# A decoder layer on one core: the first keys fetched by halves, and the FFN turned so that its inner features lie on partitions

## The chip, the cores and the metric

The kernel runs on one core of one Trainium2 chip. The metric is the device time of one execution in microseconds (us). TensorE (PE) multiplies, VectorE (DVE), ScalarE (ACT) and GpSimd (POOL) work elementwise, and SyncE (SP) issues most of the DMAs. Each engine runs its own instructions in order. SBUF is the on-chip memory of 128 partitions, PSUM the eight banks into which PE writes.

## The reference

Input x is 4 batches of 1024 tokens of 256 features; the context is 4 batches of 64 tokens. Everything is float32.

```
x = x + attn(LN(x))            # 16 heads of 16; softmax over 1024 keys, then / sqrt(256); biases
x = x + xattn(LN(x), ctx)      # 16 heads, 64 keys, scores / sqrt(16); biases
h = gelu(LN(x) @ T(W_fc).T)    # 1024 inner features
h = (h - mean(h)) * rsqrt(var(h) + 1e-5) * ln_w + ln_b     # over the 1024
x = x + h @ T(W_proj).T
LN(v) = (v - mean) / sqrt(var + 1e-5)
T(W)  = sign(W) * min(round(|W| / (mean|W| + 1e-6)), 1)    # entries -1, 0, 1
```

## The kernel before, in words

**Numbers in two parts.** Where a fast float32 product is wanted, a number is written as a rounded part and a rest (`hT` and `hl`, `xh` and `xl`), and both parts are multiplied.

**Start.** `load_x(0, 4)` (line 100) fetches batch 0 in four parts on SP's queue, then the query and key weights. `ln1(0)` normalises eight blocks of 128 tokens (lines 324 to 339), transposes them on PE into `xnT`, and `project(0, 0)` (line 341) makes queries and keys of the first eight heads. Their two parts are written to DRAM (`kept_q`, `kept_k`), and `fetch(u)` (line 368) reads them back in the layout that one unit needs: four heads, as two pairs, each of 64+64 rows. For each pair and side it issues four DMAs of 16 rows. On SP's queue a DMA also waits until an earlier one that holds the same semaphore has landed; for unit 0 half of the key DMAs are issued by ACT.

**Units.** There are 16 units (a batch and four heads). `maxima(u)` (line 412) multiplies queries by keys for 128 queries and 512 keys at a time, and DVE reduces each PSUM bank to a maximum (line 433). `turn_maxima` transposes these. In the main loop a step handles 128 keys and 512 queries: `scores` (line 872) multiplies the other way round, subtracts the maxima by a second product, and ACT takes the exponential (line 888); `weigh` (line 796) multiplies with the values. The maxima of the next unit run in the same steps. Sixteen maxima pieces of unit 0 come ahead of the loop (lines 861 to 864), with pieces of `values(0)` and `project(0, 1)` between them.

**Order.** PE and SP keep the order of the program (`ordered`). On the other engines a planner in the framework sets the order, so that an instruction may stand far ahead of its place in the program. Side work (`ln1`, `project`, `values` of the next batches; `post(b)`: output projection, cross attention and its norms; the weights' `ternary`) is written as generators, in three lines `due`, `later` and `aside`, that the steps advance by credits. `post(3)` is left over for the end.

**FFN** (lines 962 to 1106). The tokens are taken in eight halves of 512. `widen(i)` normalises four blocks, transposes them into `xh`, `xl`, and multiplies with the ternary `wfc`: per block of 128 tokens eight products of 512 inner features, so that tokens lie on partitions. ACT takes Gelu (line 1001), DVE the statistics (line 1004), ACT a square root; DVE and ACT then normalise two blocks each (lines 1012 and 1015). `narrow(i)` transposes h back (line 1031), ACT and DVE split it into `hT` and `hl` with the factor `lnw` (lines 1035, 1036), and PE multiplies with `wproj` into `py`. DVE adds `py` to x (line 1052), and SP writes it out. POOL adds `yrow`, the row that the layernorm's bias makes through `wproj` (line 280); `bias_row` (line 760) computes it in the main loop. The loop at line 1083 takes a piece of `post(3)` in two of five turns, and else a piece of `widen` or `narrow` by the places in `WIDE` and `NARROW` (line 1077); from the seventh half on, `widen` waits until `post(3)` is done.

Of the kernel before, what the change touches and what calls it, by code (L numbers as in the profile page):

```python
# [10 lines left out]
F32R = mybir.dt.float32r  # L11
DRAM = bass.MemoryType.DRAM
# [9 lines left out]
P = 128  # L22
# [8 lines left out]
def decoder_layer(ctx, tc, a, out):  # L31
# [39 lines left out]
    def load_x(b, n=1, view=x_view, slot=None):  # L71
        step = NT // n
        x_of[b] = x_slots[b % 3 if slot is None else slot]
        for i in range(n):
            sl = slice(i * step, (i + 1) * step)
            dma(
                out=x_of[b][:, sl, :], in_=view[:, b * NT + i * step : b * NT + (i + 1) * step, :]
            )
# [21 lines left out]
    load_x(0, 4)  # L100
    wqk = []
    for name in ("wq", "wk"):

        wide = main.tile([P, E // P, H, 32], F32, tag="q", name=f"{name}_in", bufs=4)
        dma(out=wide, in_=a[name].rearrange("(c p) (h e) -> p c h e", p=P, e=32))
        t = const.tile([P, E // P, H, D], F32, name=name)
        nc.gpsimd.tensor_copy(t, wide[:, :, :, 1 : 1 + D])
        wqk.append(t.rearrange("p c h e -> p c (h e)"))
# [13 lines left out]
    bo = load_row("bo")  # L122
    xbv = load_row("xbv")
    xbo = load_row("xbo")
# [37 lines left out]
    for i in range(3):  # L162
        t = (const if i else main).tile([P, NT, VW], F32, tag=f"v_sb{i}", name=f"v_sb{i}")
        nc.gpsimd.memset(t, 16.0)
        v_sb.append(t)

# [14 lines left out]
    state = {"split": False, "banks": "ring"}  # L181
# [47 lines left out]
    def ln_stats(pool, mv, blocks):  # L229

        for i, t in blocks:
            st = pool.tile([P, 6], F32, tag="bn", name="bn", bufs=3)
            nc.vector.bn_stats(out=st, in_=xs(t)[:, 0, :])  # L233
            nc.vector.bn_aggr(out=mv[:, i, :], in_=st)

    def ln_rstd(pool, rs, mv):
# [3 lines left out]
        nc.vector.reciprocal(out=rs, in_=sd)  # L240

    def ln_normalised(pool, mv, rs, i, t, n):
# [12 lines left out]
        for k in range(n):  # L255
            nc.vector.tensor_scalar(  # L256
                xn[:, k, :], xs(t + k)[:, 0, :], mv[:, i + k, 0:1], rs[:, i + k : i + k + 1],
                ALU.subtract, ALU.mult,
            )
# [108 lines left out]
    def fetch(u):  # L368
# [4 lines left out]
        for pair in range(2):  # L373
# [17 lines left out]
            for n in range(2):  # L391
                parts(k, kept_k, (0, 1, 0, 1), n, slice(0, S), dma if u or n else nc.scalar.dma_start)
# [19 lines left out]
    def maxima(u):  # L412
# [4 lines left out]
        for half in range(2):  # L417
            order = [(t, pair) for t in range(half * 4, half * 4 + 4) for pair in range(2)]
            if u == 0 and half == 0:

                order.sort(key=lambda at: at[1])
            for t, pair in order:
                q, k = qk_of[u][pair]
                for kh in range(2):
                    sides = two_banks()
                    for n, pm in enumerate(sides):
                        r = slice(64 * n, 64 * n + 64)
                        matmul(
                            pm, lhsT=q[r, t * P : (t + 1) * P],
                            rhs=k[r, kh * 512 : (kh + 1) * 512], start=True, stop=True,  # L430
                        )
                    for n, pm in enumerate(sides):
                        nc.vector.tensor_reduce(  # L433
                            mx[:, t, 2 * pair + n : 2 * pair + n + 1, kh], pm, AX.X, ALU.max
                        )
                    if kh == 1 and (t, pair) == order[-1]:
                        turning.append(turn_maxima(u, mx[:, half * 4 : half * 4 + 4, :, :]))
                    yield
# [281 lines left out]
    yrow = const.tile([P, E], F32, name="yrow")  # L720

# [37 lines left out]

    def bias_row():  # L760

        yield "free"
        wide = main.tile([P, HID // P, P], F32, tag="hl", name="lnb_wide", bufs=2)
        nc.gpsimd.tensor_copy(
            wide, late["lnb"].rearrange("p (c o) -> p c o", o=1).to_broadcast([P, HID // P, P])
        )
        yield "cols"
        pt = bank()
        w = ternaries[1].bitcast(F32)
        product(pt[:, 0:E], [(wide[:, c, :], w[:, c, :]) for c in range(HID // P)])  # L770
        nc.vector.tensor_copy(yrow, pt[:, 0:E])
# [50 lines left out]

    first, parts = ln1(0), project(0, 0)
    for _ in range(6):
        next(first)
# [4 lines left out]
    state["split"] = True  # L830
# [27 lines left out]

    due.add(values(0), 8)
    due.add(project(0, 1), 8)  # L860
    for i in range(16):
        top()
        if i % 3 != 0 and i < 15:
            due.step()
    run(turning.popleft())
    due.credit = 0.0
    load_x(1)
# [23 lines left out]
    for u in range(NU):  # L891
# [5 lines left out]
        if g == 0:  # L897
# [4 lines left out]
            for n in ((1, 2), (), (3,), ())[b]:  # L902
                if n > 1:
# [11 lines left out]
        if g == 1 and b == B - 1:  # L915
            aside.add(ternary("wfc", 2, HID), 10)
            aside.add(ternary("wproj", HID // P, E), 10)
            aside.add(bias_row(), 2)
        for step in range(2 * NT):
            half, kb = divmod(step, NT)  # L920
            if step < 2 and u + 1 < NU:
# [51 lines left out]
    h_of = {}  # L973
    NH = NT // 2

    def widen(i):
# [10 lines left out]
        h = ffn.tile([P, NH, HID], F32, tag="h", name="h", bufs=2)  # L987
        mv = ffn.tile([P, NH, 2], F32, tag="mvh", name="mvh", bufs=2)
        rs = ffn.tile([P, NH], F32, tag="rsh", name="rsh", bufs=2)
        h_of[i] = h  # L990
        for t in range(NH):
            yield "Gelu"
            ph = ps["wide"]()
            for half in range(2):
                for k in range(4):
                    c, part = divmod(k, 2)
                    matmul(
                        ph[:, half, :], lhsT=(xl, xh)[part][:, c, t * P : (t + 1) * P],
                        rhs=wfc[:, c, half * 512 : (half + 1) * 512], start=k == 0, stop=k == 3,
                    )  # L1000
            nc.scalar.activation(h[:, t, :], ph.rearrange("p a f -> p (a f)"), AF.Gelu)  # L1001
            st = ffn.tile([P, 2, 6], F32, tag="bnh", name="bnh", bufs=3)
            for half in range(2):
                nc.vector.bn_stats(out=st[:, half, :], in_=h[:, t, half * 512 : (half + 1) * 512])  # L1004
            nc.vector.bn_aggr(out=mv[:, t, :], in_=st)
        yield "Sqrt"
        ln_rstd(ffn, rs, mv)
        nmr = ffn.tile([P, NH], F32, tag="nmr", name="nmr", bufs=2)
        nc.vector.scalar_tensor_tensor(nmr, mv[:, :, 0], -1.0, rs, ALU.mult, ALU.mult)
        for t in range(0, NH, 2):  # L1010
            yield ""
            nc.vector.tensor_scalar(
                h[:, t, :], h[:, t, :], mv[:, t, 0:1], rs[:, t : t + 1], ALU.subtract, ALU.mult
            )
            nc.scalar.activation(
                h[:, t + 1, :], h[:, t + 1, :], AF.Identity, bias=nmr[:, t + 1 : t + 2],
                scale=rs[:, t + 1 : t + 2],
            )

    def narrow(i):  # L1020


        h = h_of.pop(i)
        t0 = i * NH
        py = ps["wide"]()
        parts = []
        for c in range(HID // P + 2):
            if c < HID // P:
                pt = bank()
                for n in range(NH):  # L1030
                    transpose(pt[:, n * P : (n + 1) * P], h[:, n, c * P : (c + 1) * P], ident)
                hT = ffn.tile([P, 512], F32R, tag="hT", name="hT", bufs=4)
                hl = ffn.tile([P, 512], F32R, tag="hl", name="hl", bufs=4)
                w = late["lnw"][:, c : c + 1]
                nc.scalar.activation(hT, pt, AF.Copy, scale=w)  # L1035
                nc.vector.scalar_tensor_tensor(hl, pt, w, hT.bitcast(F32), ALU.mult, ALU.subtract)  # L1036
                parts.append((hl, hT))
            if c >= 2:
                for k, part in enumerate(parts[c - 2]):
                    for n in range(NH):  # L1040


                        matmul(
# [120 lines left out]
```

## Time and profile before

| | us |
|---|---|
| three runs, median (lowest, highest) | 1367.08 (1364.13, 1367.55) |
| the profiled execution | 1365.17 |
| its span | 1363.4 |
| PE busy | 1282.1 (94%) |
| DVE busy | 1004.7 (74%) |
| ACT busy | 898.5 (66%) |
| POOL busy | 80.0 (6%) |

Busy shares are averages over stages with different limits, so they say little by themselves; a stage is read from the table of busy times by stretches and from what its engines wait for. A line of the timeline gives the start, the length, the engine, the line of the kernel, the operation with what it writes and reads, the count, and in brackets the idle time before it with what ended it. "issue" there means that no releaser is seen in the profile. Matmul ends are modelled and overlap, so the pitch from start to start is used for PE. `PEld` is PE's weight load.

### The profile page before, as it was taken

To read this page: it belongs to the slowest core of one execution; us is meant where nothing else is said; L and a number is where in the kernel's file an instruction comes from. 1 tells how busy PE (TensorE), PEld (TensorE's weight loads), DVE (VectorE), ACT (ScalarE), POOL (GpSimd) and SP (SyncE) were. 2 spreads that over 40 slices of the span, in tenths; PEclk is the share of its full clock that TensorE was granted. 3 is DMA by queue.
4 is the path that set the end of the run, shared out by engine and by line. 5 is a ranking of instruction groups with operands and counts; after the bars stand their busy time and mean duration, and the time that the engine had idled before them with its cause. 6 is when DMAs were issued, how large, how long until landed. Compare 5 with 4: busy or idle time off the path is not lost.

```text
span 1363.4 us, 27651 instructions
## 1 busy us (share of the span) xinstructions
PE 1282.1 (94%) x11000; PEld 717.4 (53%) x11000; DVE 1004.7 (74%) x2110; ACT 898.5 (66%) x1654; POOL 80.0 (6%) x86
## 2 busy tenths in 40 slices
PE   3879999999999999999999999999999988999987
PEld 1434445545545454444545544545455466776777
DVE  4877777867878877877877777878889357565665
ACT  1377666756687667777676676676766746474765
POOL 4000000003010000011000000010000012000000
PEclk9889999999999999989999999999999989999989
DMA  5440312312130202131212112212210010100000
GB/s 169 126 143 30 111 42 68 94 48 63 41 85 1 63 7 57 33 93 31 64 35 60 38 27 75 82 53 73 55 40 1 2 62 1 44 19 31 1 31 32
DMA packets 46064, 72.72 MB, mean 53 GB/s; under 512 B 11280, under 2 KB 27920, under 8 KB 45936
## 3 DMA queue, kind: packets, MB, share of 16 engines
q1 hardware_dynamic: 44720, 68.47, 17.0%
q8 instruction: 87, 1.43, 0.4%
q10 hardware_dynamic: 1072, 2.10, 0.4%
q0 software_dynamic: 144, 0.39, 0.2%
q14 instruction: 41, 0.34, 0.1%
HBM read 46.81 MB, written 24.12 MB: 52 GB/s over the span
## 4 chain that ended last, share of the span: by engine, by line
PE 73%; DVE 16%; ACT 8%; issue 2%; DMA 1%; SPq 0%; DVEq 0%; ACTq 0%
PE ps_ring L57 42%; PE ps_acc L57 15%; PE ps_wide L57 8%; DVE mx L433 8%; PE ps_misc L57 3%; ACT exp L888 3%; PE ps_misc L60 2%; PE ps_ring L60 2%; DVE nm L592 2%; ACT xn L250 1%; DVE xn L256 1%; DVE bn L233 1%; DMA x<-in_x 1%; ACT ex L625 1%; ACT hl L359 1%
## 5 line engine op out<-in xcount | busy, mean ns | idle before, releaser
L433 DVE TENSOR_REDUCE mx<-ps_ring 128x1 f32<-128x512 f32 x1024 | 646.4, 682 | 157.6 <-PE ps_ring L57 156.7
L888 ACT ACTIVATE exp<-ps_ring 128x512 f32<-128x512 f32 x1024 | 549.2, 606 | 191.1 <-PE ps_ring L57 187.5
L57 PE MATMUL ps_ring<-q,k 64*128 64x512 f32 x1024 | 280.5, 474 | 8.0 <-ACT exp L888 5.9
L57 PE MATMUL ps_ring<-k,q 64*128 64x512 f32 x1024 | 260.2, 425 | 20.1 <-DMA q<-kept_q 7.9
L57 PE MATMUL ps_acc<-exp,v_sb 128*32 128x512 f32 x2048 | 275.3, 610 | 0.0
L57 PE MATMUL ps_ring<-mT,sel 64*128 64x512 f32 x1024 | 232.8, 400 | 0.2 <-ACT mT L451 0.2
L57 PEld LDWEIGHTS ps_ring<-q,k 64*128 64x128 f32 x1024 | 115.5, 185 | 198.4 <-ACT exp L888 69.0
L57 PEld LDWEIGHTS ps_ring<-k,q 64*128 64x128 f32 x1024 | 124.2, 186 | 100.2 <-ACT exp L888 41.3
L57 PEld LDWEIGHTS ps_ring<-mT,sel 64*128 64x128 f32 x1024 | 108.0, 186 | 6.3 <-ACT mT L451 0.7
L57 PEld LDWEIGHTS ps_acc<-exp,v_sb 128*32 128x32 f32 x2048 | 40.5, 108 | 67.4 <-issue 65.6
L1004 DVE BATCH_NORM_STATS2 bnh<-h 128x6 f32<-128x512 f32 x64 | 41.2, 679 | 34.1 <-ACT h L1001 34.0
L1001 ACT ACTIVATE h<-ps_wide 128x1024 f32<-128x1024 f32 x32 | 32.7, 1026 | 41.6 <-PE ps_wide L57 41.5
L1036 DVE SCALAR_TENSOR_TENSOR hl<-ps_misc,lnw,hT 128x512 fp32r<-128x512 f32 x64 | 46.4, 733 | 18.2 <-ACT hT L1035 18.2
L57 PE MATMUL ps_wide<-wproj,hl 128*128 128x256 f32 x256 | 46.2, 303 | 12.6 <-DVE hl L1036 12.5
L57 PE MATMUL ps_wide<-wfc,xl 128*128 128x512 f32 x128 | 56.5, 442 | 1.4 <-DVE xl L271 1.4
L57 PE MATMUL ps_wide<-wfc,xh 128*128 128x512 f32 x128 | 54.3, 424 | 0.0
L1035 ACT ACTIVATE hT<-ps_misc,lnw 128x512 fp32r<-128x512 f32 x64 | 42.6, 687 | 16.3 <-PE ps_misc L60 16.3
L233 DVE BATCH_NORM_STATS2 bn<-x 128x6 f32<-128x256 f32 x96 | 38.8, 416 | 8.1 <-DMA x<-in_x 6.4
L57 PEld LDWEIGHTS ps_wide<-wproj,hl 128*128 128x128 f32 x256 | 34.9, 191 | 16.2 <-DVE hl L1036 14.8
L280 POOL TENSOR_TENSOR x<-x,xbo 128x512 f32<-128x512 f32 x16 | 20.6, 1295 | 367.0 <-ACT xn L250 358.5
L57 PE MATMUL ps_wide<-wproj,hT 128*128 128x256 f32 x256 | 41.4, 284 | 0.0
L407 ACT COPY v_sb<-ps_ring 128x256 f32<-128x256 f32 x32 | 12.0, 375 | 41.0 <-PE ps_ring L57 30.6
(166 smaller groups left out, 1467.1 us busy)
## 6 DMA issues: line engine op xcount, KB each, us to landing
k<-kept_k SPq DMA_DIRECT2D x248, 64.0 KB
q<-kept_q SPq DMA_DIRECT2D x240, 64.0 KB
kept_q<-hl SPq DMA_DIRECT2D x15, 512.0 KB
kept_k<-hl SPq DMA_DIRECT2D x14, 512.0 KB
out<-x SPq DMA_DIRECT2D x16, 256.0 KB
x<-in_x SPq DMA_DIRECT2D x3, 1024.0 KB
x_kept<-x SPq DMA_DIRECT2D x3, 1024.0 KB
x<-x_kept SPq DMA_DIRECT2D x3, 1024.0 KB
```

Source lines behind the costliest of these rows:

```text
L57: ordered(nc.tensor.matmul(*args, **kwargs))
L60: ordered(nc.tensor.transpose(*args))
L233: nc.vector.bn_stats(out=st, in_=xs(t)[:, 0, :])
L250: nc.scalar.activation(xn[:, k, :], xs(t + k)[:, 0, :], AF.Identity, bias=nmr[:, k : k + 1], scale=rs[:, i + k : i + k + 1],)
L280: nc.gpsimd.tensor_tensor(xs(t, 2), xs(t, 2), row.rearrange("p (o d) -> p o d", o=1).to_broadcast([P, 2, E]), ALU.add,)
L433: nc.vector.tensor_reduce(mx[:, t, 2 * pair + n : 2 * pair + n + 1, kh], pm, AX.X, ALU.max)
L592: nc.vector.tensor_reduce(nm[:, t, s, :], pm[s].rearrange("p (h k) -> p h k", k=SK), AX.X, ALU.max, negate=True,)
L888: nc.scalar.activation(ex[:, n, :], pe[n], AF.Exp)
L1001: nc.scalar.activation(h[:, t, :], ph.rearrange("p a f -> p (a f)"), AF.Gelu)
L1004: nc.vector.bn_stats(out=st[:, half, :], in_=h[:, t, half * 512 : (half + 1) * 512])
L1035: nc.scalar.activation(hT, pt, AF.Copy, scale=w)
L1036: nc.vector.scalar_tensor_tensor(hl, pt, w, hT.bitcast(F32), ALU.mult, ALU.subtract)
```

## The change

**Start.** The first two parts of batch 0 are loaded, then wq, then the other two, then wk. Rows `bo`, `xbv`, `xbo` are loaded after POOL's memsets. While `pinned` is set, DVE's layernorm instructions keep the program's order, in which all eight blocks are normalised before the first products are drained. The keys of unit 0 are fetched in halves of 512 columns, and the first maxima go through the first half of the keys before the second. Four pieces of `project(0, 1)` are run before the first maxima; eight of the sixteen maxima pieces are followed by a piece of side work. `fetch(1)` is issued ahead of `load_x(1)`, not in the first steps of unit 0, and `load_x(2)` in unit 1.

**FFN.** `widen` takes a block of 128 inner features of `wfc` as the stationary side and 512 tokens as the moving side, so inner features lie on partitions and h needs no transposes. ACT makes Gelu, then `hT` (times `lnw`, which is now one number per partition) and the square of h. DVE makes `hl` and a running sum of h over the eight blocks, POOL a running sum of the squares. At the end of a half the two sums are transposed (8 transposes) and reduced on DVE to sums per token; POOL works out mean, variance and the inverse root by three Newton steps (`ln_root`). `narrow` multiplies the unnormalised parts with `wproj`; mean and inverse root come in afterwards: x gains `crow` times -mean*rs and `py` times rs. `yrow` and `crow` (the same row for `lnw`) are computed at the start of the FFN, and `bias_row` is gone. `post(3)` gets four of nine turns; `widen` has seven pieces instead of nine, `narrow` eight instead of nine.

```diff
-    load_x(0, 4)
+    load_x(0, 4, parts=(0, 1))
...
+        if name == "wq":
+            load_x(0, 4, parts=(2, 3))
...
-            nc.vector.bn_stats(out=st, in_=xs(t)[:, 0, :])
-            nc.vector.bn_aggr(out=mv[:, i, :], in_=st)
+            pinned(nc.vector.bn_stats(out=st, in_=xs(t)[:, 0, :]))
+            pinned(nc.vector.bn_aggr(out=mv[:, i, :], in_=st))
...
+    def ln_root(pool, rs, mv):
+        n = mv.shape[1]
+        by = pool.tile([P, 4, n], F32, tag="root", name="root", bufs=2)
+        var, half, t, nmr = (by[:, i, :] for i in range(4))
+        engine = nc.gpsimd
+        engine.tensor_scalar(var, mv[:, :, 1], 0.0, LN_EPS, ALU.max, ALU.add)
+        engine.tensor_scalar(half, var, -0.5, None, ALU.mult)
+        engine.tensor_scalar(
+            rs.bitcast(I32), var.bitcast(I32), -0.5, float(0x5F3759DF), ALU.mult, ALU.add
+        )
+        for _ in range(3):
+            engine.tensor_tensor(t, rs, half, ALU.mult)
+            engine.tensor_tensor(t, t, rs, ALU.mult)
+            engine.tensor_scalar(t, t, 1.5, None, ALU.add)
+            engine.tensor_tensor(rs, rs, t, ALU.mult)
+        engine.tensor_tensor(nmr, mv[:, :, 0], rs, ALU.mult)
+        engine.tensor_scalar(nmr, nmr, -1.0, None, ALU.mult)
+        return nmr
...
-            for n in range(2):
-                parts(k, kept_k, (0, 1, 0, 1), n, slice(0, S), dma if u or n else nc.scalar.dma_start)
+            for cols in halves:
+                for n in range(2):
+                    parts(k, kept_k, (0, 1, 0, 1), n, cols, dma if u or n else nc.scalar.dma_start)
...
-                order.sort(key=lambda at: at[1])
-            for t, pair in order:
+                order.sort(key=lambda at: at[1:])
+            for at in order:
+                t, pair, kh = at
...
     first, parts = ln1(0), project(0, 0)
-    for _ in range(6):
+    for _ in range(10):
         next(first)
...
+    parts = project(0, 1)
+    for _ in range(5):
+        next(parts)
...
     due.add(values(0), 8)
-    due.add(project(0, 1), 8)
+    due.add(rest_of(parts), 4)
     for i in range(16):
         top()
-        if i % 3 != 0 and i < 15:
+        if i % 2 == 0:
             due.step()
     run(turning.popleft())
     due.credit = 0.0
+    run(fetch(1))
     load_x(1)
...
-                if n > 1:
+                if n > 2:
                     load_x(n)
...
-            aside.add(bias_row(), 2)
...
+            if u == 1 and step == 2:
+                load_x(2)
-            if step < 2 and u + 1 < NU:
+            if step < 2 and 0 < u < NU - 1:
...
+        sums = ffn.tile([P, 2, 512], F32, tag="sums", name="sums", bufs=2)
+        last = None
+        for c in range(HID // P):
+            if c % 2 == 0:
+                yield "Gelu"
+            ph = bank()
+            for k in range(4):
+                f, part = divmod(k, 2)
+                matmul(
+                    ph, lhsT=wfc[:, f, c * P : (c + 1) * P], rhs=(xl, xh)[part][:, f, :],
+                    start=k == 0, stop=k == 3,
+                )
...
+            nc.scalar.activation(h, ph, AF.Gelu)
+            w = late["lnw"][:, c : c + 1]
+            nc.scalar.activation(hT, h, AF.Copy, scale=w)
+            nc.scalar.activation(sq, h, AF.Square)
+            nc.vector.scalar_tensor_tensor(
+                hl, h, w, hT.bitcast(F32), ALU.mult, ALU.subtract
+            )
+            if last is not None:
+                before = last if c == 1 else (sums[:, 0, :], sums[:, 1, :])
+                nc.vector.tensor_tensor(sums[:, 0, :], before[0], h, ALU.add)
+                nc.gpsimd.tensor_tensor(sums[:, 1, :], before[1], sq, ALU.add)
+            last = h, sq
...
+        for k in range(2):
+            pt = bank()
+            for n in range(NH):
+                transpose(pt[:, n * P : (n + 1) * P], sums[:, k, n * P : (n + 1) * P], ident)
+            nc.vector.tensor_reduce(
+                total[:, k, :], pt.rearrange("p (n k) -> p n k", n=NH), AX.X, ALU.add
+            )
...
+        shift_of[i] = rs, ln_root(ffn, rs, mv)
...
+            if c in (3, 5):
+                for n in range(c - 3, c - 1):
+                    row = xs(t0 + n)[:, 0, :]
+                    nc.vector.scalar_tensor_tensor(
+                        row, crow, nmr[:, n : n + 1], row, ALU.mult, ALU.add
+                    )
+        for n in range(NH):
+            row = xs(t0 + n)[:, 0, :]
+            nc.vector.scalar_tensor_tensor(
+                row, py[:, n // 2, n % 2 * E : (n % 2 + 1) * E], rs[:, n : n + 1], row, ALU.mult,
+                ALU.add,
+            )
...
-        if tag is not None and turn % 5 in (0, 2):
+        if tag is not None and turn % 9 in (0, 2, 4, 6):
```

## The prediction

> **What bounds the kernel now.** I read the busy table by stage first, then the chain that ended last, then the timeline where a stage had gaps. Columns: stretch, length, busy time of PE, weight load, DVE, ACT, POOL (with counts), granted clock, DMA.
>
> ```profile
> 0.00:34.16 34.16, 12.96 (x33) 6.32 (x33) 14.92 (x43) 6.76 (x11) 13.93 (x20) 0.94 0.55 169
> 34.16:57.70 23.54, 19.44 (x192) 8.06 (x192) 20.73 (x37) 3.94 (x10) 0.00 (x0) 0.86 0.26 66
> ...
> 80.00:100.00 20.00, 11.79 (x90) 5.31 (x87) 13.06 (x45) 15.05 (x25) 2.78 (x16) 0.74 0.55 166
> ```
> ```profile
> 1101.80:1273.40 171.60, 156.04 (x929) 117.26 (x929) 109.54 (x233) 101.32 (x136) 20.79 (x16) 0.96 0.07 25
> 1273.40:1298.40 25.00, 22.55 (x144) 19.99 (x144) 21.20 (x46) 21.20 (x26) 2.69 (x2) 1.00 0.00 1
> 1298.40:1322.80 24.40, 21.49 (x136) 19.07 (x136) 16.98 (x31) 16.32 (x21) 2.67 (x2) 0.93 0.07 22
> 1322.80:1363.40 40.60, 33.31 (x232) 30.47 (x232) 22.15 (x38) 18.68 (x25) 0.00 (x0) 0.93 0.12 40
> ```
>
> Between 100 and 1100 us PE is busy 95% and more; the change hardly touches that. It touches four places: the start (0 to 34 us: DMA and setup; 34 to 57.7: DVE's maxima, 32 reductions at 0.62), the hole at 80 to 100 us, the end of the main loop, and the FFN: a mixed stage (the last batch's `post` with five half-batches, PE busy 91%), then three half-batches with no other work beside them.
>
> ```profile
> 29.17 6.13 ACTq L383 DMA_DIRECT2D k<-kept_k  x8
> 34.16 1.42 PE L57 MATMUL ps_ring<-k,q 64*128 64x512 f32 x4 [7.93 <-DMA q<-kept_q]
> ...
> 85.75 4.03 ACT L250 ACTIVATE xn<-x,nmr,rs 128x256 f32<-128x256 f32 x8
> 91.43 0.20 DVE L240 RECIPROCAL rs<-sd 128x8 f32<-128x8 f32 x1 [3.96 <-ACT sd L239]
> 93.88 1.34 PE L57 MATMUL ps_ring<-k,q 64*128 64x512 f32 x2 [7.24 <-issue]
> ...
> 1097.15 3.64 PE L57 MATMUL ps_ring<-wproj,lnb_wide 128*32 128x256 f32 x64
> ```
> In the timeline the first maxima stand 7.93 us for the fetched keys. In the hole ACT normalises batch 1 (eight at 0.50), then loads Sqrt for batch 2; DVE sits behind that in its own order, so no bank is freed and PE stands 7.24 us.
>
> **The start: -5 us (-8 to +1).** DVE now has its first four rows' statistics, reciprocal and normalisation ahead of the second half's, which wait for DMA (before, the first normalisation stood until 10.97). But the first split key and query products still come behind the second half's normalisation on DVE, and that half's x now lies behind wq (0.5 MB, 2.5 us at the 207 GB/s of the first slice). The gain at the first writes to DRAM is therefore about 3 us: the first key half issued near 19.6 instead of 22.45, the second near 22.9 instead of 26.05. A write took 3.1 us to release its fetch (26.05 to 29.16). With halves, the first fetch waits for the first write only: 19.6+3.1=22.7 instead of 29.16, first maxima about 27.5 instead of 34.16. Against it: 32 key fetches for 16. SP gains 8 at 0.51 (8.16 for 16 in the same queue), 4 us; ACT gains 8 at up to 0.77, and four projection drains of the second group stand behind ACT's sixteen issues, each holding a bank, with DVE's subtractions and the value drains behind those. I put ACT free at 33 to 35, DVE's remaining 24 reductions and 4 subtractions at 24x0.62+4x0.47=16.8, so the maxima end near 52, not 57. The three row loads leave the head of POOL's queue (0.69+0.54+0.54): the identity is ready 1.8 earlier, and their first readers are after 75 us.
>
> **Unit 0: -6 us (-9 to -1).** Two projection pieces (16 records, 1.0 each) leave the PE-bound loop for the idle start: -2. Fetch of the second group goes ahead of x of batch 1: 32 issues at 0.5 are 16 us on SP, so x lands about 70, when its first statistics ran before (68.87). x of batch 2 is loaded in unit 1, so its Sqrt and table loads (1.28+0.30+1.28) leave the hole; batch 1's normalisation stays. Of 8.2 us lost there I take back half, 4; it comes back in part where batch 2 is normalised.
>
> **Bias row: -3.6, +1.** The 64 records at 1097.15 lie alone on PE: 3.64 away. In the FFN 32 products for two rows take their place at 0.118 each, 3.8, in front of a gap of 2.03+0.67 before the first FFN products: +1.
>
> **FFN, PE.** From the chain, eight transposes, eight products by wfc, eight by wproj:
>
> ```profile
> 1280.85 0.87 PE ps_misc L60 x8
> 1281.73 1.86 PE ps_wide L57 x8
> ...
> 1284.03 0.94 PE ps_wide L57 x8
> ```
> The products keep their number. Per half 32 transposes go (3.5) and 8 come for the sums (0.9): -2.6, so the mixed stage needs 156.0-5x2.6=143 of PE; at 91% that is 157.
>
> **FFN, ACT.** Per feature block: Gelu 0.52 (the exponentials' pitch, 2.07 for four), a scaled copy and a square that now read SBUF. Rows: 512 elements lie between 0.50 (256, L250) and 1.18 (1024, L1015): 0.73. The Trainium skill (VectorE: DVE Perf Modes, the errata section) has 224+512 cycles at 1.2 GHz, 0.61. By the row a block is 1.9 to 2.0, 15.5 a half; by the rule 14. I take the row. Before: four Gelu, two identities, eight copies and two table loads, about as much. ACT is no bound.
>
> **FFN, DVE and POOL.** DVE per half, at pitch: eight `hl` 0.66 (L755, two for 1.41), seven adds 0.66, four crow and four result rows 0.40 (L317), two sums and two `xl` 0.60, four `xn` 0.36: 17.0, the same as now. POOL gets seven adds at 1.28 and a chain of 21 small operations. And here a row speaks against the change:
>
> ```profile
> 1053.19 1.41 DVE L755 SCALAR_TENSOR_TENSOR wproj<-raw,thr,neg 128x512 fp32r<-128x512 f32 x2
> 1054.66 1.23 POOL L764 COPY lnb_wide<-lnb 128x1024 f32<-128x1024 f32 x1 [143.56 <-DVE wproj L755]
> 1055.03 1.41 DVE L755 SCALAR_TENSOR_TENSOR wproj<-raw,thr,neg 128x512 fp32r<-128x512 f32 x1
> ```
> One DVE instruction with two SBUF inputs takes as long beside a POOL copy as two alone. A single row could be chance; the Trainium skill (SBUF — State Buffer, Who interferes with whom) makes it a lock: a DVE instruction with two SBUF inputs and a POOL instruction that reads SBUF exclude each other for a whole instruction. `hl`, the adds and crow are all of that kind now; `hl` used to read PSUM. Without the lock DVE's block is 1.3 and ACT's 1.9 sets the pace; with it a half needs 8x0.66+7x0.66+7x1.28=18.9 in its loop.
>
> The small POOL operations have no near row: from below 0.10 (a 128x1 memset), from above 0.35 (start to start of two dependent memsets, 13.10 and 13.45). The skill's two-input add of 2048 elements (GPSIMD Engine Reference, 3.1) takes 4.50 and the trace's of 512 1.28, which leaves 0.21 at no elements: an estimate. I take 0.25, chain 5.3 (2.1 to 7.4). Behind it on DVE stand the crow rows, and behind them, in order, the next half's `hl`, for which PE's wproj products wait.
>
> *Mixed stage, -8 (-15 to +5):* DVE 109.5 plus at most 35 new POOL adds x1.28=45 is 155; at 91% 170. PE alone gave 157. I take the middle, 163.5.
> *The last three halves, 0 (-16 to +7):* loop 18.9, then transposes 0.9, sum 0.6, chain 5.3, crow 1.6: 27.3 a half, twice, against 25.0+24.4: +5.2. The last: first block 2.8, loop 18.9, transposes 0.9, eight pairs of wproj products at 0.95 with the chain under them 7.6, rows and output 5.2: 35.4 against 40.6, -5.2, since no normalisation stands between the two products any more.
>
> **Sum:** -5-6-3.6+1-8+0=-21.6. The profiled execution took 1365.17 (1363.4 of it span); the median shown is 1.9 above it. 1365.2-21.6+1.9=1345.5.
>
> **Rivals.**
> *No lock worth speaking of* (0.20): DVE's idle third absorbs the waits. Mixed 157; a half is ACT's 15.5 plus 6 to refill, 21.5 twice (-6.4), the last 32 (-8.6): tail -29.6, 1324. For it: DVE idles 36% of the mixed stage. Against: the row above.
> *The start gives nothing* (0.12): ACT's sixteen issues and DVE's order eat the halves, and the hole stays: -11 is lost, 1356.
> *Slower* (0.17): POOL's chain holds DVE. Crow waits for its last operation, everything on DVE waits for crow. Seven halves pay it; each 0.1 us per operation costs 2.1 a half, 14.7 in all. The gain is gone at 0.40 per operation and the kernel slower by over 0.3% from 0.43; at 0.5 it takes 1382. Against: 0.35 is the largest step the trace shows, and `post` can fill the waits in five halves.
> *As forecast* 0.51.
>
> **How the numbers follow.** 0.3% (4 us) is about what this kernel's measurement can tell. The forecast, the free lock and the empty start all end faster, less their upper edges: 0.76. Same 0.07, from the forecast's worst terms and the mild end of the chain; slower 0.17. The range reaches from the free lock to below the chain's 1382: 1322 to 1373.
>
> **What would show it.** First maxima near 27 us; the hole at 80 to 100 us halved; in the FFN `hl` and the adds well above 0.74 wherever a POOL add overlaps; undisturbed halves of about 27 us from one sums transpose to the next; POOL's small operations near 0.25. Wrong if ACT ends the waits of PE there, if halves are at 22 or above 31, or if the new start only moves the wait to the drains behind ACT's issues.

## The result, and the profile after

Against the kernel before, 1366.38 us (median of four runs), the changed kernel took 1412.78 us (1411.5 to 1414.9): a ratio of 1.034, interval 1.0327 to 1.0358. It is slower by 46 us where 21.6 us less was forecast. Its profiled execution took 1411.5, 1409.7 of it span.

Busy time by stage of the changed kernel (stretch, length, then busy time of PE, weight load, DVE, ACT, POOL with counts, granted clock, DMA share, GB/s):

```profile
0.00:31.28 31.28, 15.47 (x96) 7.82 (x97) 17.38 (x43) 6.55 (x11) 13.67 (x20) 0.96 0.57 173
31.28:57.70 26.42, 23.06 (x160) 9.09 (x160) 18.33 (x31) 4.07 (x11) 0.00 (x0) 0.66 0.45 130
...
80.00:100.00 20.00, 15.06 (x112) 6.85 (x113) 15.81 (x43) 15.43 (x29) 1.50 (x8) 0.83 0.22 71
1092.00:1313.00 221.00, 167.03 (x893) 123.29 (x894) 151.78 (x237) 110.42 (x185) 97.17 (x156) 0.87 0.06 20
1313.00:1340.30 27.30, 16.96 (x103) 15.25 (x102) 26.96 (x39) 16.25 (x27) 14.43 (x9) 0.86 0.03 11
1340.30:1369.30 29.00, 19.28 (x113) 17.45 (x113) 25.61 (x31) 15.33 (x26) 18.79 (x30) 0.79 0.05 16
1369.30:1396.30 27.00, 18.63 (x114) 16.76 (x113) 22.72 (x28) 15.48 (x26) 15.11 (x28) 0.88 0.06 20
1396.30:1409.70 13.40, 8.28 (x65) 8.07 (x64) 4.41 (x10) 0.00 (x0) 4.40 (x21) 0.88 0.19 65
```

The main loop ends near 1092, before it ended at 1101.8: 9.8 us are gained up to there. The mixed stage (the last batch's `post` with five half-batches, until the fifth half's shift is known) takes 221 us, not 171.6: 49.4 lost. The rest takes 96.7 for 90.0: 6.7 lost. The sum is 46.3. So the loss is in the FFN, and nearly all of it in the mixed stage. Both kernels do nearly the same products there: all of `post`, the wide products of five halves and the narrow ones of four.

What PE waited for in the FFN of the changed kernel, with the total, the number of waits and the longest:

```profile
PE ps_misc L61 <- DVE sums L1045: 48.1, 7, 10.3
PE ps_misc L58 <- ACT xn2T L302: 9.2, 2, 8.3
PE ps_misc L61 <- DVE attx L332: 5.0, 1, 5.0
```

The first line is the transposes of the running sums, one set per half; 20.2 of its 48.1 us lie in the mixed stage and 27.9 in the last three halves. One such place in the timeline of the changed kernel:

```profile
1202.71 0.51 PE L58 MATMUL ps_misc<-xl,wfc 128*128 128x512 f32 x1
...
1206.55 0.60 PE L61 MATMUL ps_misc<-ident,oT 128*128 128x128 f32 x4
1209.99 3.09 DVE L1045 TENSOR_TENSOR sums<-sums,h 128x512 f32<-128x512 f32 x2
1211.21 0.63 ACT L1039 ACTIVATE sq<-h 128x512 f32<-128x512 f32 x1
1213.13 2.24 PE L61 MATMUL ps_misc<-ident,sums 128*128 128x128 f32 x8 [5.98 <-DVE sums L1045]
...
1222.24 1.47 DVE L1090 SCALAR_TENSOR_TENSOR x<-crow,root,x 128x256 f32<-128x256 f32 x1 [3.08 <-POOL root L270]
1224.10 1.54 PE L61 MATMUL ps_misc<-ident,attx 128*128 128x128 f32 x6 [5.05 <-DVE attx L332]
```

PE makes four feature blocks' wide products in 3.8 us (from 1202.71). For the same four blocks ACT needs until 1211.84 and DVE's last add until 1213.08; PE's next instruction but one needs that add, and stands 5.98. Then `post`'s `attx` on DVE stands behind a crow row, which stands for POOL's chain, and PE stands another 5.05.

Such a wait is paid twice. Around the wait of 7.17 us that ends at 1123.84, the same columns by short stretches:

```profile
1116.60:1123.80 7.20, 0.06 (x1) 0.00 (x0) 7.20 (x12) 2.67 (x6) 3.16 (x2) 0.58 0.00 0
1123.80:1126.00 2.20, 2.16 (x10) 2.10 (x11) 1.52 (x4) 0.00 (x0) 0.24 (x1) 0.50 0.00 0
1126.00:1128.00 2.00, 2.00 (x6) 1.64 (x5) 0.51 (x1) 0.00 (x0) 1.28 (x6) 0.52 0.00 0
1128.00:1130.00 2.00, 2.00 (x13) 1.75 (x13) 1.33 (x4) 0.59 (x1) 1.43 (x7) 1.00 0.00 0
```

For some 4 us after the wait the granted clock is 0.50, and PE works at half speed. After the 8.32 us wait that ends at 1153.04 it is 0.50 for 5.6 us. In the mixed stage as a whole PE's idle time rose from 15.6 to 54.0 us (+38.4), and its busy time from 156.0 to 167.0 (+11.0). By the trace's clock record PE was busy at half clock for 13.0 us of this stage before and for 34.9 after. Counted as half, they leave 149.6 us of work at full speed in both kernels, so the 11 us are the clock's. Idle time and clock together are the 49.4.

The lock, in an undisturbed half of the changed kernel:

```profile
1350.33 0.67 DVE L1045 TENSOR_TENSOR sums<-h 128x512 f32<-128x512 f32 x1
...
1354.33 1.78 DVE L1040 SCALAR_TENSOR_TENSOR hl<-h,lnw,hT 128x512 fp32r<-128x512 f32 x1
1356.04 1.78 DVE L1045 TENSOR_TENSOR sums<-sums,h 128x512 f32<-128x512 f32 x1
...
1353.94 10.01 POOL L1046 TENSOR_TENSOR sums<-sums,sq 128x512 f32<-128x512 f32 x6
```

Six POOL adds take 1.67 each, and beside them every DVE operation with two SBUF inputs takes 1.75 to 1.78: they take turns, one for one.

At the start, from the timeline of the changed kernel:

```profile
27.95 8.19 ACTq L416 DMA_DIRECT2D k<-kept_k  x13
31.28 0.76 PE L58 MATMUL ps_ring<-k,q 64*128 64x512 f32 x1 [4.95 <-DMA k<-kept_k]
36.24 0.84 ACT L392 ACTIVATE hl<-ps_ring,bq_c 128x256 fp32r<-128x256 f32 x2 [11.32 <-DMA q<-kept_q]
64.01 1.58 ACT L919 ACTIVATE exp<-ps_ring 128x512 f32<-128x512 f32 x3
...
91.87 1.34 PE L58 MATMUL ps_ring<-k,q 64*128 64x512 f32 x2 [4.39 <-issue]
```

The first maxima begin at 31.28 (before 34.16), but ACT issues key fetches until 36.14, the drains of the second group's projection stand behind them, and the first exponential comes at 64.01, where it came at 60.43. The hole of 7.24 us that ended at 93.88 is 4.39 now.

PE's clock is part of the late start. From the first maxima until the clock was back, in the changed kernel and then in the kernel before:

```profile
31.28:49.30 18.02, 14.79 (x78) 5.40 (x78) 10.13 (x18) 2.58 (x7) 0.00 (x0) 0.50 0.34 89
34.16:40.10 5.94, 5.94 (x40) 2.31 (x40) 3.77 (x6) 0.38 (x2) 0.00 (x0) 0.50 0.49 125
```

Half of the 14.79 busy us is lost to the clock, 7.4, where before it was half of 5.94, 3.0. Between the first maxima PE waits some 0.8 us at a time, for DVE's reductions or a fetch; before, it had no wait in this stretch.

### The profile page after: what moved, and what is told of

Read it like the earlier page. It is cut to its first block, busy times and chain, and to the rows that moved or that the text cites. A ratio compares the mean times of both kernels' runs of the same rounds, so it can differ in the third digit from the quotient of the medians.

```text
span 1409.7 us, 27621 instructions
## 1 busy us (share of the span) xinstructions
PE 1276.6 (91%) x10776; PEld 710.7 (50%) x10776; DVE 1068.2 (76%) x2107; ACT 897.2 (64%) x1713; POOL 202.1 (14%) x309
## 4 chain that ended last, share of the span: by engine, by line
PE 64%; DVE 19%; ACT 7%; issue 4%; POOL 3%; DMA 2%; SPq 0%; DVEq 0%; POOLq 0%; ACTq 0%
PE ps_ring L58 42%; PE ps_acc L58 15%; DVE mx L469 6%; PE ps_misc L58 3%; DVE sums L1045 3%; ACT exp L919 2%; PE ps_ring L61 2%; DVE hl L1040 2%; DVE nm L628 2%; PE ps_wide L58 1%; ACT xn L281 1%; DVE bn L242 1%; DVE xn L288 1%; DMA x<-in_x 1%; DVE x L1090 1%
## 5 line engine op out<-in xcount | busy, mean ns | idle before, releaser
L1046 POOL TENSOR_TENSOR sums<-sums,sq 128x512 f32<-128x512 f32 x48 | 73.6, 1532 | 66.7 <-ACT sq L1039 64.5
L1040 DVE SCALAR_TENSOR_TENSOR hl<-h,lnw,hT 128x512 fp32r<-128x512 f32 x64 | 76.1, 1198 | 3.9 <-ACT hT L1038 3.5
L1045 DVE TENSOR_TENSOR sums<-sums,h 128x512 f32<-128x512 f32 x48 | 56.6, 1179 | 16.2 <-ACT h L1036 15.4
L1036 ACT ACTIVATE h<-ps_misc 128x512 f32<-128x512 f32 x64 | 36.8, 592 | 36.2 <-PE ps_misc L58 31.5
L61 PE MATMUL ps_misc<-ident,sums 128*128 128x128 f32 x64 | 14.4, 391 | 48.7 <-DVE sums L1045 48.1
L58 PE MATMUL ps_misc<-xl,wfc 128*128 128x512 f32 x128 | 53.1, 415 | 3.0 <-DVE xl L304 2.9
L313 POOL TENSOR_TENSOR x<-x,bo 128x512 f32<-128x512 f32 x16 | 19.9, 1281 | 239.7 <-ACT xn L281 210.5
L313 POOL TENSOR_TENSOR x<-x,yrow 128x512 f32<-128x512 f32 x16 | 22.3, 1398 | 219.2 <-DMA x<-x_kept 192.0
L58 PE MATMUL ps_misc<-xh,wfc 128*128 128x512 f32 x128 | 50.8, 397 | 0.0
L1038 ACT ACTIVATE hT<-h,lnw 128x512 fp32r<-128x512 f32 x64 | 46.2, 723 | 1.0
```

The costliest lines, as they stand in the source:

```text
L58: ordered(nc.tensor.matmul(*args, **kwargs))
L61: ordered(nc.tensor.transpose(*args))
L313: nc.gpsimd.tensor_tensor(xs(t, 2), xs(t, 2), row.rearrange("p (o d) -> p o d", o=1).to_broadcast([P, 2, E]), ALU.add,)
L1036: nc.scalar.activation(h, ph, AF.Gelu)
L1038: nc.scalar.activation(hT, h, AF.Copy, scale=w)
L1040: nc.vector.scalar_tensor_tensor(hl, h, w, hT.bitcast(F32), ALU.mult, ALU.subtract)
```

## The experiments

**Which part loses.** The first part alone: the changed kernel's start and main loop, with the FFN and bias row of before.

```
-  (FFN of the change)
+  (widen, narrow, bias_row, WIDE/NARROW of before)
```

> The kernel before with the change's first part alone (keys by halves, all rows normalised first, second group's fetch first, projection pieces earlier), and the FFN of before with its bias row. The trace of the changed kernel reaches its FFN 9.9 us earlier, and 3.6 of that is the bias row, which this one keeps. Theory (the whole loss lies in the FFN, the first part keeps what it gains): 1366.4-9.9+3.6 = 1360, 1357 to 1363. Rival (the gain is only moved, and the last batch's work or its fetches give it back): 1365 to 1368.

Measured: 1361.53 beside 1365.14 of before, ratio 0.997 (0.9961 to 0.998). As the theory had it, near its number; against the changed kernel it is 51 us less. The first part gains a little; the FFN, with its rows in place of the bias row, loses 51.

**The order on PE.** The sums' transposes, reductions and chain are moved behind the third feature block of the narrow product.

```
+            if c == 2:
+                totals(i)              # transposes, reductions, chain
-            if c in (3, 5):            # crow rows
+            if c in (5, 6):
```

> The changed kernel, with the transposes of the running sums, their two reductions and POOL's chain moved from the end of a half's wide product to behind the third feature block of its narrow product; crow's rows follow two blocks later. Same operations, same engines. Theory PE's order (PE stands 48 us at these transposes, with post's work queued behind them): PE's wait goes, at least 30 of the 48 us come back, 1370 to 1383. Rival, lock alone (DVE beside POOL's adds sets the pace wherever the transposes stand): DVE's stretched operations stay, 1403 to 1413.

Measured: 1411.12, 1.7 less than the changed kernel, about what two sets of runs of the kernel before differ by (1365.1 and 1366.4). PE's wait at the transposes went, as asked, but not the time. The waits in its FFN, PE's and then one of DVE:

```profile
PE ps_misc L58 <- DVE xl L304: 30.2, 4, 15.7
PE ps_misc L61 <- DVE nm L628: 8.2, 2, 4.9
PE ps_misc L61 <- DVE attx L332: 8.1, 2, 6.3
PE ps_misc L61 <- DVE sums L1045: 7.9, 1, 7.9
...
DVE x L1095 <- POOL root L270: 42.8, 8, 6.9
```

48.1 became 7.9, and 30.2 appeared at the next half's `xl`, with `nm` and `attx` of `post` after it. All four of PE's lines wait for something that DVE makes, so moving one instruction only moved the wait. The theory that this one place was the cause falls.

**The lock.** One word, at line 1046: DVE adds the squares.

```
-                nc.gpsimd.tensor_tensor(sums[:, 1, :], before[1], sq, ALU.add)
+                nc.vector.tensor_tensor(sums[:, 1, :], before[1], sq, ALU.add)
```

> The changed kernel with the running sum of the squares added by DVE instead of POOL, nothing else moved. In the changed kernel 64 hl at 1.198 and 56 adds at about 1.13 take 140 us of DVE; at 0.74 and 0.68 they take 85, and 56 more adds of 0.68 cost 38. Theory lock: DVE is 15 us less busy, and the operations no longer stretch: hl at 0.74, adds at 0.68, no half above 27, 1390 to 1398. Rival, no lock (the stretch has another cause, such as ACT's own SBUF accesses): hl stays above 1.1 and the time rises by the 38 us of adds, to 1430 and more.

Measured: 1400.04, 12.7 less. The groups of its FFN:

```profile
L1040 DVE SCALAR_TENSOR_TENSOR hl<-h,lnw,hT 128x512 fp32r<-128x512 f32 x64 | 51.4, 804 | 5.2 <-ACT hT L1038 4.8
L1045 DVE TENSOR_TENSOR sums<-sums,h 128x512 f32<-128x512 f32 x48 | 33.9, 705 | 17.0 <-ACT h L1036 16.6
L1046 DVE TENSOR_TENSOR sums<-sums,sq 128x512 f32<-128x512 f32 x48 | 32.9, 685 | 0.0
```

`hl` fell from 1198 to 804 ns and the adds from 1179 to 705: the lock is real, and an offload to POOL cost more than doing the adds on DVE. The time is 2 us above the theory's range (1390 to 1398), and one half, 31.5 with the end of `post` in it, stayed above 27. Where the 12.7 lie is telling: undisturbed halves went from 29.6 and 27.0 to 26.1 and 23.7, the mixed stage only from 212 to 210 (counted from the two rows' first product to the fifth half's sums). By itself, the lock is not what made the mixed stage long.

**Both together.**

> Both edits at once: transposes of the sums behind the third narrow block, and the squares added by DVE. If the order on PE and the lock are separate costs, they add up: 1353 to 1370, near the kernel before. If each only uncovers the other (DVE is the bound in any case), it is no better than the better of the two by more than 5 us.

Measured: 1392.88: 7.2 below the better of the two. That is far from the range in which they were to be two separate costs, and just outside the other statement: moving the transposes is worth 1.7 with the lock and 7.2 without it. The mixed stage shows it: 213 with the transposes late, 210 without the lock, 202 with both. So the lock costs 11 us of this stage once the transposes no longer hide it.

**The PSUM ring.** The wide product now takes its banks from the ring that `post` uses.

```
-    open_psum("wide", 2, [P, 2, 512]); open_psum("misc", 4, [P, 512])
+    open_psum("wide", 1, [P, 2, 512]); open_psum("misc", 6, [P, 512])
```

> The changed kernel with PSUM divided otherwise in the FFN: one two-bank tile for the narrow product instead of two, six banks in the common ring instead of four. In the changed kernel the wide product takes its banks from that ring, beside post, the transposes and the sums. Theory ring (PE stands because the next bank in the ring is still held by an operation deep in ACT's or DVE's queue): at least 15 us back, below 1398, the waits spread less over PE. Rival (PE stands for the data itself, through the order of DVE and ACT): within 4 us of 1412.8, or slower because a narrow product now waits for the rows before it.

Measured: 1410.29, 2.5 less: the rival. PE still stands 50.4 us at the transposes of the sums; banks are not what it waits for.

**POOL's chain.** `engine = nc.vector` in `ln_root`, and the four operations before it likewise.

> The changed kernel with the chain of 21 small operations (mean, variance, root, shift) on DVE instead of POOL. Theory of the slower rival (POOL's chain holds DVE, which stands 21.7 us before crow's first rows): at 0.06 to 0.1 us an operation on DVE a chain takes 1.3 to 2.1 us instead of 6.0 and the eight chains give 15 to 30 us, 1383 to 1398. Lock and queues: only the three undisturbed halves and some of the others gain, 4 us each: 1398 to 1408.

Measured: 1407.99, 4.8 less, at the edge of the second range. An operation took 0.16 to 0.30 on DVE, not 0.06 to 0.1, and DVE's busy time in the FFN rose by some 23 us; DVE's stand of 21.7 us before crow is gone. The chain is worth 5 us, not the cause.

**The amount of elementwise work.** First without the running sums from the third block on, then without ACT's squares as well.

```
-            if last is not None:
+            if c == 1:
                 (adds of h and of sq)
...
-            nc.scalar.activation(sq, h, AF.Square)
+            if c < 2:
+                nc.scalar.activation(sq, h, AF.Square)
```

> Left out: the running sums beyond the second feature block, so no adds of h or of squares by DVE or POOL after that (the statistics are wrong by it). The squares are still made. DVE is 54-64 us less busy and the lock is gone. Theory elementwise burst (DVE's and ACT's work of a half now all stands in the wide product, and PE waits behind it): the mixed stage falls from 221 to below 195, the halves to 20 to 23; 1362 to 1380. Rival (the order in which the program lists post, wide and narrow pieces makes the gaps): the mixed stage stays above 205, only the last three halves shorten: 1385 to 1395.

> As the run before, and ACT's squares beyond the second block are left out as well (48 at 0.62 us, 30 us of ACT). If ACT is the next bound of a half once the adds are gone (1.94 us a block, 15.5 a half), the halves fall by 3 to 4 us more each, and the total by 10 to 25. If PE's order sets the rest: less than 5.

Both leave out most of the statistics, so their results are wrong; they measure time alone. Measured: 1368.44, 44.3 less than the changed kernel, and 1342.02, another 26.4. The theory of the elementwise burst holds in both, and the second gain is just above its range. The mixed stage of the second, and its last three halves:

```profile
1092.00:1264.00 172.00, 147.61 (x858) 107.58 (x856) 106.18 (x203) 93.05 (x152) 49.89 (x105) 0.98 0.09 28
1264.00:1340.70 76.70, 63.38 (x428) 57.74 (x426) 53.80 (x95) 40.89 (x67) 29.45 (x91) 0.98 0.08 28
```

With nothing but Gelu, `hT` and `hl` from the third block on, PE's clock is at 0.98, the stage takes 172 up to the fifth half's sums, where the changed kernel takes 214 (from 1092 to 1306), and the last two halves take 19.4. What the statistics need in this layout, placed as the change places it, costs 71 us. This kernel is also 19.5 below the first part alone, but the FFN of before makes its statistics, so what the products by features save by themselves is not shown.

**Its place.** On the run with DVE's squares, `hl` is made in the narrow product again, one block ahead.

```
+        def low():
+            h, hT = parts.popleft()
+            nc.vector.scalar_tensor_tensor(hl, h, w, hT.bitcast(F32), ALU.mult, ALU.subtract)
+        low()
         for c in range(HID // P):
+            if parts:
+                low()
```

> The changed kernel with the squares added by DVE, and in addition hl made in the narrow product, one block ahead of the product that reads it, instead of in the wide one. The same operations; DVE's 0.74 per block is only moved to where before had it. The run with the squares on DVE alone took 1400.0. Theory burst (what counts is how much elementwise work stands between one wide product and the next things PE needs): 8 to 20 us less, 1380 to 1392. Rival (the amount counts, not its place): 1397 to 1403.

Measured: 1390.42, 9.6 less than without the move, with the same operations. The mixed stage takes 193 instead of 210; part of these 17 us comes back in the last halves and behind them, where `hl` now stands. Place counts.

**All placements at once**: squares and chain on DVE, `hl` in the narrow product, transposes late.

> The changed kernel with every placement found so far at once: the squares added by DVE, hl made in the narrow product, the sums' transposes behind the third narrow block, the small chain on DVE. Same mathematics. If the parts add up (12.7 for the squares' adds, 9.6 for hl, 7 for the transposes once the lock is gone, 5 for the chain): 1412.8-34.5 = 1378, 1373 to 1384, and the rest over the kernel before is the amount of elementwise work, above all the squares on ACT. If place is everything and they help one another: below 1368. If they overlap: 1386 to 1391.

Measured: 1371.42 beside 1366.38, ratio 1.0045 (1.003 to 1.0059), between two of the stated ranges. The parts do a little more than add up (41 us, not 34.5), and the time is 29 above the kernel without most of the statistics, not 71. Against the first part alone some 10 us stay, with DVE busy 229.6 us of the FFN where before it was 169.9: I take them for the amount, though no run isolates these 10. ACT's busy time is no larger than before (157.6 against 157.5), so ACT's squares, which the expectation put first, have not made ACT's amount larger.

The stages of these runs, from the timelines: the mixed stage from the two rows' first product to the fifth half's reductions, and the three pitches from one half's reductions to the next (in the rows with late transposes the reductions stand three narrow blocks later). The first pitch holds the end of `post`; the other two are undisturbed.

| | mixed | three halves |
|---|---|---|
| changed kernel | 212 | 33.4, 29.6, 27.0 |
| transposes late | 213 | 34.9, 31.0, 23.2 |
| squares on DVE | 210 | 31.5, 26.1, 23.7 |
| both of these | 202 | 34.9, 25.8, 19.3 |
| squares on DVE, `hl` in narrow | 193 | 32.1, 27.0, 23.5 |
| no running sums | 189 | 24.4, 23.2, 19.3 |
| nor squares | 169 | 24.2, 19.5, 19.3 |
| all placements | 191 | 28.8, 20.6, 19.4 |

**The first part, taken apart** (FFN of before in all three). Keys whole and maxima in the old order, the rest of the first part kept; then only the new order of fetches and the early projection pieces; then keys by halves with the second halves issued by SP.

```
 keys whole:    the loop "for cols in halves" and the order by (t, pair, kh) undone
 fetches only:  kept of the change: run(fetch(1)) ahead of load_x(1), load_x(2) in unit 1,
                next(parts) x5 of project(0, 1), the rows bo/xbv/xbo after the weights
 by SP:         dma if u or n or cols.start else nc.scalar.dma_start
```

> The first part alone (FFN of before), but the first keys fetched whole and the first maxima in their old order; rows normalised first, projection pieces early and second group's fetch first stay. With halves the trace shows the first maxima at 31.3 instead of 34.2, but ACT busy with thirteen key fetches to 36.2, the four drains of the second group behind them, and the first exponential 3.6 us later than before. Theory (the sixteen issues on ACT's queue undo the halves): without them the first exponential comes at or before 60.4 and the time is 1356 to 1360. Rival (the halves help, and something else in the start is late): 1362 to 1366.

> The kernel before with only the second group's fetch ahead of batch 1, batch 2's x in unit 1, two projection pieces before the maxima and the row loads behind the weights; keys whole, rows normalised in the old order, FFN of before. In the changed kernel unit 0 gains 7.7 us from its first exponential to the first of unit 1, and another 2 by unit 3. Theory: nearly all of it is here: 1356 to 1361. Rival (it depends on the earlier start, or the old start delays these pieces): 1363 to 1367.

> The first part alone (FFN of before), keys by halves, but only the first halves issued by ACT: the second halves' eight go to SP. ACT is free of fetches about 5 us earlier, SP's queue holds eight more at 0.5. Theory (ACT's issues hold the drains): the first exponential 2 to 4 us earlier than with all on ACT, 1357 to 1360. Rival (the keys' own arrival sets it): 1361 to 1364.

Measured, beside 1365.71: keys whole 1355.13 (0.9922, 0.991 to 0.9934), fetches only 1354.58 (0.9925, 0.9912 to 0.9938), by SP 1356.57 (0.9929, 0.9917 to 0.994). With both halves on ACT it was 0.997. All three are just below their theories' ranges. So issuing the second halves on ACT costs some 5.6 us (by SP, 0.9929, against 0.997), and whole keys are no worse than halves; the new order of normalisation shows nothing (the first two agree); and the order of fetches with the early pieces and the later rows, alone, gives the whole gain. PE's clock goes with it: behind the first maxima it is 0.50 until 49.3 in the changed kernel, until 51.9 in the first part alone, and until 37.0 to 39.5 in these three. No run separates the drains that wait behind ACT's issues from the clock. **"Fetches only" is faster than both kernels**, by 10 to 11 us against before.

Where it gains shows in the start of the same exponentials (of 1024, 64 a unit), against before's, worked out from the timelines:

| exponential (before's start) | changed | first part alone | fetches only |
|---|---|---|---|
| 1st (60.43) | +3.6 | +6.1 | -1.8 |
| 25th (92.71) | +2.1 | +4.7 | -3.3 |
| 33rd (104.02) | -3.5 | -0.9 | -8.8 |
| 65th, unit 1 (133.86) | -4.7 | -2.1 | -10.1 |
| 257th (323.38) | -6.0 | -3.4 | -11.3 |
| 1021st (1095.96) | -7.6 | -2.9 | -10.3 |

All three gain 5.5 us between the 25th and the 33rd, in the hole at 80 to 100 us; they differ by the start. The changed kernel and the first part alone have the same instructions in the same order up to the first exponential, and yet their traces differ by 2.5 us there: a single trace places the start no better than that. The two stretches around it in "fetches only":

```profile
57.70:80.00 22.30, 22.30 (x188) 11.54 (x190) 19.54 (x34) 15.36 (x30) 1.49 (x8) 0.93 0.62 194
80.00:100.00 20.00, 15.06 (x108) 6.99 (x104) 15.59 (x45) 15.76 (x30) 1.51 (x8) 0.83 0.12 35
```

PE is busy 15.06 of the 20 us, where before it was 11.79.

## Why the prediction was wrong

**Mixed stage, -8 against +49: the step that failed.** "PE alone gave 157", "DVE ... is 155; at 91% 170 ... I take the middle". DVE's amount was nearly right: 151.8 us busy up to 1313. What failed is dividing an amount by PE's 91%. DVE was full in bursts and empty between, 69% over the stage, because the change moves the work in time: `hl`, the squares and both adds now all stand in the wide product. A block gives PE 0.94 us of products, ACT 1.6 (6.57 for the four blocks shown) and DVE 1.3, or 3.4 when both of its operations meet a POOL add (starts 1.71 apart), so PE runs ahead and then meets, in its fixed order, an instruction that needs the end of DVE's queue. The runs show the amount (-71 without sums and squares), the place (-9.6 for `hl`), and that neither the lock (-2 in this stage by itself, -11 with the transposes late) nor one wait nor the banks is the cause alone. PE's own term was mis-sized too: of the forecast -13 nothing came. Its work at full speed is 149.6 in both, since the transposes of only four halves, not five, stood in the stage before, and the two rows' 32 products came in.

**The price of a wait.** No term of the sum had the clock: 11.0 of the mixed stage's 49.4, and 4.4 more at the start. Two waits with the time behind them, the first in the kernel before, the second in the changed one:

```profile
1197.90:1200.20 2.30, 0.01 (x1) 0.00 (x0) 2.30 (x7) 2.00 (x3) 0.70 (x1) 1.00 0.00 0
1200.20:1200.70 0.50, 0.49 (x4) 0.50 (x5) 0.50 (x2) 0.02 (x1) 0.00 (x0) 0.97 0.00 0
1200.70:1204.10 3.40, 3.40 (x11) 2.77 (x10) 2.88 (x5) 3.05 (x4) 1.28 (x1) 0.50 0.00 0
1188.20:1190.90 2.70, 0.00 (x0) 0.00 (x0) 1.80 (x2) 2.64 (x4) 2.62 (x2) 1.00 0.00 0
1190.90:1195.00 4.10, 4.08 (x23) 2.31 (x24) 0.00 (x0) 1.09 (x3) 0.29 (x1) 1.00 0.00 0
```

The Trainium skill (TensorE: Matmul & The Clock Gate, Part 1: The HAM clock gate) states that about 3.4 us of idling bring PE to half its clock, and that it takes about as long busy to come back. The long waits fit: 0.50 for 4.1 and 5.6 us after waits of 7.17 and 8.32, which costs 2 to 2.8 us more. The short ones do not: a wait of 2.29 us was followed by 3.4 us at 0.50, one of 2.74 by none. The measurement decides: in these traces the length of a wait alone does not tell, and one well short of 3.4 us can cost 1.7 us more than itself.

**Last three halves, 0 against +6.7.** Loop and half were nearly right: by the stretches above 27.3, 29.0 and 27.0, for two of 27.3 and a last one of 22.6 before its reductions. The last half was mis-sized: I let it begin with nothing in front, but the chain (6.04, forecast 5.3) and crow of the half before stand there too. POOL's add was 1.67 under the lock, not 1.28. The end after the sums, 13.4 for 12.8, was right. The lock was the right mechanism: taking POOL's adds out gives back 3.5 and 3.3 us in the two undisturbed halves.

**Start, -5 against +3.6.** "ACT gains 8 at up to 0.77 ... I put ACT free at 33 to 35": it was 36.1, and the step that failed is what stands around it. The first key fetch was issued at 22.12 (forecast 22.7), but ACT's next two only at 26.50, after the second key write (23.80) and a drain of queries (24.23) in its order, so the first maxima came forward by 2.9 of the forecast 6.7. DVE's reductions then came singly, with waits between them, until 47, with PE at half clock; the forecast had 24x0.62 for them, without waits or clock. That the drains behind ACT's issues are the cause is argued from the queue; the runs with fewer issues on ACT bear it out as far as ACT's issues go, not as to drains or clock. This was the mechanism of the rival "the start gives nothing"; it decided the sign of the start, not of the whole.

**Unit 0, -6 against -8.3** (from +3.6 to -4.7 at unit 1). Right, undersized: the hole gave 5.5, not 4. **Bias row, -3.6 and +1**: the loop did lose its 3.64; the 32 products of the two rows took 5.4, not 3.8, with the clock at 0.50 for the first 3.2 us of it.

**The rivals.** "No lock" is out by the 1.75 us operations. The slower one named POOL's chain; its operations have a pitch of 0.29, below the 0.40 from which it decides, and moving them gives 4.8. The chance of 0.17 had the right side by luck, for the wrong reason. Of the signs named for reading the trace, the first maxima near 27 us failed (31.28) and the others were seen: the hole nearly halved, halves of 29.6 and 27.0, `hl` above 0.74, small operations at 0.29. The last three were signs for the undisturbed halves; for the mixed stage, which held the larger term, I had named none.

## What to carry to other kernels

When work moves from one generator to another, add up per piece what each engine gets from it, not per stage: a piece that gives PE 0.9 us, ACT 1.6 and DVE up to 3.4 makes PE wait in its order, however idle those engines are on average. Price PE's clock with the waits: here it was 11 of 49 us. A layout that saves transposes but puts the reduced axis on partitions turns one statistics instruction into a square and two adds; price these first. Before dividing a DMA fetch into more issues, look at which engine issues them and what it drains next.

## What the runs showed of the hardware

- After waits of 7.17 and 8.32 us PE ran at a granted clock of 0.50 for 4.1 and 5.6 us; after one of 2.29 us for 3.4 us, after one of 2.74 us not at all.
- With waits of some 0.8 us between short bursts the clock stayed at 0.50 for 18 us, though PE was busy for 14.79 of 18.02 us.
- Operations of DVE with two SBUF inputs and POOL adds alternated one for one: 0.67 to 0.75 alone, 1.75 beside a queue of POOL adds, which themselves take 1.67 instead of 1.28.
- A POOL operation on 128x4 elements took 0.19 to 0.24 at a pitch of 0.29, on DVE 0.16 to 0.30: moving the chain gave 4.8 us over eight halves.
- An ACT operation of 512 elements from SBUF with a scale per partition took 0.72, the square of the same tile 0.62.
